# A vision tower on one NeuronCore: first attention with the query projections of two chunks in one set of matmuls

## The chip, the core and the metric

One core of a Trainium2 chip runs the whole program. The time is device microseconds of one execution; the median of several runs counts. The engines work side by side, each down its own list of instructions: TensorE (PE, matmuls; PEld is its weight load), VectorE (DVE), ScalarE (ACT), GpSimd (POOL), and SyncE (SP), which starts DMAs. An instruction waits for results of other engines by semaphores.

## The reference

The network takes 128 images, cuts each into 64 tokens of 256 features by two convolutions, and sends them through two layers of attention and feed-forward blocks. Only the attention of the first layer is touched:

```python
Q, K, V = x @ Wq.T, x @ Wk.T, x @ Wv.T            # x: (128, 64, 256), normalized
Qg = Q.reshape(B, L, 1, G, Dg)                    # G = 8 groups of Dg = 32
Kg = K.reshape(B, 1, L, G, Dg)
attn = einsum('bqkgd,d->bqkg', relu(Qg - Kg), w_mlp) + b_mlp[0]
attn = softmax(relu(attn), axis=2)
out = einsum('bqkg,bkdg->bqdg', attn, V.reshape(B, L, Dg, G))
```

The costly part is relu(q - k): for each image, each pair of a query and a key, and each of 256 features there is one subtraction and one relu, and then a weighted sum over 32 features.

## The kernel before, in words

Images are taken in eight blocks of 16 (NB = 16). A block's 64 queries per image are taken 8 at a time, so a block has eight chunks, and there are 64 chunks in all. I call a chunk by its place in its block, c0 to c7, which is its number modulo 8. Features lie on the partitions: 256 of them make two halves (hf = 0 and 1).

For one chunk, each of 16 images and each half, a tile of 8 queries x 64 keys is made, and three engines share that work. For images 0 to 7 of both halves, and 12 and 13 of half 1, VectorE takes max(q, k) (`larger`, L532; the missing -k is put in once per block as a key sum, L439 to L452, and enters through `begin`, L525). It reads the queries straight from their PSUM tile. For images 8 to 15 of half 0 and 8 to 11 of half 1, GpSimd subtracts (`difference`, L540) and ScalarE does the relu (L541). For images 14 and 15 of half 1 ScalarE does all of it, a query at a time (`by_query`, L550). GpSimd and ScalarE read the queries from a copy in SBUF that ScalarE makes (`queried`, L472). TensorE sums over features: each tile of 512 columns goes through one matmul with 32 output rows (`summed`, L342), four of them side by side, into the scores `sc`.

The scores of a chunk are finished in the course of the next chunk: VectorE takes their maximum and subtracts it (`less_max`, L566 to L568), ScalarE takes the exponent (L573), VectorE sums (L576), GpSimd scales (L580), TensorE transposes (L589), ScalarE copies (L597).

The order of all engines is written out by hand in one loop over the chunks, L696 to L757. It has named places (`do(n, "X")`, "A", "Y", "B", "Z", "O", "C", "W", "V1", "V2") into which other work is put by chunk number: the projections of the next block, the output of the last one. What matters here, in the order of a chunk on TensorE:

- the last sums of the chunk before, then the first sums of this one: three sets of four matmuls
- place X
- two more sets, which need the relu of the second difference
- the queries of the next chunk (`queries`, L454): four matmuls of 128 columns into a tile `pc`
- place Y
- three more sets, `begin` for the next chunk, the transposition, place Z.

In X are key projections (`keys`, L403, at c4 and c5) and value projections (`values`, L421, at c6 and c7), their copies on ScalarE at place A; a second set of values is in Y with copies at B, and key projections for the other eight images in Z.

Query tiles `pc` are in a pool of two PSUM buffers. A tile holds 2 x 16 x 8 queries, and 8 columns more into which `less_max` puts its maximum (L565). Parts from VectorE have a pool of three buffers of four images (`mvp`), differences one of five (`mgp`); projections and transposed tiles share four PSUM buffers (`sh.ps`).

Of the kernel before, what the change touches and what calls it, by code (L numbers as in the profile page):

```python
# [12 lines left out]
F32 = mybir.dt.float32  # L13
# [7 lines left out]
P = 128  # L21
B = 128
# [37 lines left out]
def bcast(ap, axis, n):  # L60

    v = ap.unsqueeze(axis)
    shape = list(v.shape)
    shape[axis] = n
    return v.to_broadcast(shape)
# [243 lines left out]
def relu_attention(c, sh, wqkv, wmlp, bmlp, beside):  # L309
# [6 lines left out]
    tc, nc, h2 = c.tc, c.nc, c.h2  # L316
    NB = 16
    NP = NB // 2
    np_, bp, atp, ep = sh.np_, sh.bp, sh.atp, sh.ep
    with (  # L320
# [29 lines left out]
        class Block:  # L350


            def __init__(self, b0):
                self.b0, self.p0 = b0, b0 // 2
                self.pc, self.q, self.ps = {}, {}, {}
# [97 lines left out]

            def queries(self, q0):  # L454

                self.pc[q0] = pc = psc.tile([P, 2 * NB * 8 + 8], F32, tag="pc", name="pc")
                pq = pc[:, : 2 * NB * 8].rearrange("p (c i t) -> p c i t", c=2, i=NB)
                xi = self.xT.rearrange("p c n (b t) -> p c (n b) t", b=2)
                for fo in range(2):
                    for fi in range(2):  # L460
                        nc.tensor.matmul(
                            pq[:, fo],
                            w[:, fi, fo * P : (fo + 1) * P],
                            xi[:, fi, :, q0 : q0 + 8],
                            start=(fi == 0),
                            stop=(fi == 1),
                        )

            def queried(self, q0):
                self.q[q0] = q = ep.tile([P, 2, NB // 2, 8], F32, tag="q", name="q")  # L470
                pq = self.pc[q0][:, : 2 * NB * 8].rearrange("p (c i t) -> p c i t", c=2, i=NB)
                nc.scalar.copy(q, pq[:, :, NB // 2 :])  # L472


            def outcome(self, hf):
# [36 lines left out]
        class Chunk:  # L512


            def __init__(self, blk, q0):
                self.blk, self.q0, self.parts, self.m = blk, q0, {}, {}
                self.pc = blk.pc.pop(q0)
                self.pq = self.pc[:, : 2 * NB * 8].rearrange("p (c i t) -> p c i t", c=2, i=NB)
                self.q = blk.q.pop(q0)

            def begin(self):
# [40 lines left out]
            def less_max(self):  # L562
                self.e = e = ep.tile([P, 8, T], F32, tag="e", name="e")
                self.mx = mx = ep.tile([P, 8], F32, tag="mx", name="mx")
                pm = self.pc[:, 2 * NB * 8 :]  # L565
                nc.vector.tensor_reduce(pm, self.sc, AX.X, ALU.max)  # L566
                nc.vector.tensor_scalar_max(mx, pm, 0.0)
                nc.vector.scalar_tensor_tensor(  # L568
                    e, self.sc, 0.0, bcast(mx, 2, T), ALU.max, ALU.subtract
                )  # L570
# [32 lines left out]
        def at(n, place, *steps):  # L603
            work.setdefault((n, place), []).extend(steps)

        def of(f, *a):
            return lambda: f(*a)
# [26 lines left out]
        for b, x in enumerate(blocks):  # L634
            n = 8 * b

            if b + 1 < len(blocks):
                at(n + 9, "X", of(x.outcome, 0))
                at(n + 9, "A", of(x.outcome_copied, 0, 0))
                at(n + 9, "B", of(x.outcome_copied, 0, 1))  # L640
                at(n + 9, "Y", of(x.outcome, 1))
                at(n + 9, "C", of(x.outcome_copied, 1, 0))
                at(n + 10, "O", of(x.outcome_copied, 1, 1))
                for i in range(4):
                    at(n + 10 + i // 2, "XY"[i % 2], of(x.back, i))
                    at(n + 10 + i // 2, ("V1", "V2")[i % 2], of(x.added, i))
            if b == 0:
                for i in range(4):
                    at(i // 2 * 2, "XY"[i % 2], of(x.values, i))
                    at(i // 2 * 2, "AB"[i % 2], of(x.valued, i))  # L650
                continue

            if b == 1:
                at(0, "V1", *(of(x.statistics, i) for i in range(NP)))
                at(0, "W", x.factors)
                at(0, "C", of(x.normal, 0), of(x.normal, 1))
                at(1, "X", of(x.transpose, 0))
                at(1, "A", of(x.normal, 2), of(x.transposed, 0))
                at(1, "B", of(x.normal, 3))
                at(1, "Z", of(x.transpose, 1))  # L660
                at(2, "O", of(x.transposed, 1))
            else:
                for i in range(NP):
                    at(n - 21 + i if b > 2 else 1 + i // 4, "V2", of(x.statistics, i))
                at(n - 15 if b > 2 else 2, "W", of(x.factors, 0, 4))
                at(n - 10, "W", of(x.factors, 4, 8))
                for i in range(4):
                    at(n - 12 + i, "C", of(x.normal, i))
                at(n - 8, "X", of(x.transpose, 0))
                at(n - 8, "A", of(x.transposed, 0))  # L670
                at(n - 8, "Z", of(x.transpose, 1))
                at(n - 7, "O", of(x.transposed, 1))
            for i in range(2):
                at(n - 6 + i, "A", of(x.normal, 4 + 2 * i))
                at(n - 6 + i, "B", of(x.normal, 5 + 2 * i))
                at(n - 6 + i, "Z", of(x.transpose, 2 + i))
                at(n - 5 + i, "O", of(x.transposed, 2 + i))
            for fo in range(2):
                at(n - 4 + fo, "X", of(x.keys, 0, fo))
                at(n - 4 + fo, "A", of(x.keyed, 0, fo))  # L680
                at(n - 4 + fo, "Z", of(x.keys, 1, fo))
                at(n - 3 + fo, "O", of(x.keyed, 1, fo))
            at(n - 2, "Y", x.key_sums)
            at(n - 1, "V1", x.correction)
            for i, (k, place) in enumerate(((6 - (b == 1), "Y"), (4, "Y"), (2, "X"), (1, "X"))):
                at(n - k, place, of(x.values, i))
                at(n - k, "BA"[place == "X"], of(x.valued, i))

        for (n, place), steps in beside.items():
            at(n, place, *steps)  # L690
# [5 lines left out]
        with tc.manual_schedule():  # L696
            seq = [(x, q0) for x in blocks for q0 in range(0, T, 8)]
            first(blocks[0])
            ch, old = Chunk(*seq[0]), None
            for n in range(len(seq)):  # L700
                new = None
                ch.difference(8, 0)
                ch.larger(mvp, 0, 4, 0)
                do(n, "O")
                if n == 0:
                    first_rest(blocks[0])
                    ch.begin()
                ch.by_query(14, 1, 0)
                ch.add(0, 0)
                do(n, "X")  # L710
                ch.difference(10, 0)
                ch.add(8, 0)
                ch.larger(mvp, 4, 4, 0)
                ch.add(4, 0)
                if old:
                    old.less_max()
                    old.exponents()
                ch.by_query(14, 1, 1)
                if n + 1 < len(seq):
                    seq[n + 1][0].queries(seq[n + 1][1])  # L720
                ch.difference(8, 1)
                do(n, "A")
                do(n, "V1")
                do(n, "Y")
                ch.difference(10, 1)
                if n + 1 < len(seq):
                    seq[n + 1][0].queried(seq[n + 1][1])
                    new = Chunk(*seq[n + 1])
                do(n, "B")
                ch.by_query(15, 1, 0)  # L730
                ch.add(8, 1)
                ch.larger(mvp, 0, 4, 1)
                ch.add(0, 1)
                if old:
                    old.sums()
                ch.difference(12, 0)
                if old:
                    old.weights()
                do(n, "W")
                ch.by_query(15, 1, 1)  # L740
                ch.larger(mvp, 4, 4, 1)
                ch.add(4, 1)
                if new:
                    new.begin()
                if old:
                    old.transpose()
                do(n, "Z")
                ch.larger(mgp, 12, 2, 1)
                do(n, "V2")
                ch.difference(14, 0)  # L750
                if old:
                    old.transposed()
                do(n, "C")
                ch.add(12, 0)
                ch.add(12, 1, True)
                old, ch = ch, new
            old.less_max()  # L757
# [1569 lines left out]
```

## Time and profile before

| | us |
|---|---|
| median of 3 runs | 2665.02 |
| the runs | 2665.02, 2655.38, 2665.51 |
| the profiled execution | 2654.66 |
| its span, first to last instruction | 2652.9 |
| first attention, about 195 to 1083 | 888 |

In the first attention a block of eight chunks takes about 110.3 us. These are its costliest groups there (line, engine, operation, what it writes and reads, count, busy time and mean ns of one, then idle time of the engine just before and who ended it):

```profile
L540 POOL TENSOR_TENSOR m<-q,k 128x1024 f32<-128x1024 f32 x384 | 719.6, 1907 | 55.9 <-PE sc L342 46.8 <-ACT q L472 8.9
L532 DVE TENSOR_TENSOR m<-pc,k 128x2048 f32<-128x2048 f32 x256 | 574.8, 2266 | 0.5 <-ACT q L472 0.5
L342 PE MATMUL sc<-m,wide 128*32 128x512 f32 x4096 | 520.0, 597 | 8.9 <-ACT m L541 6.6 <-DVE m L532 2.2
L541 ACT ACTIVATE m<-m 128x1024 f32<-128x1024 f32 x384 | 402.5, 1049 | 20.4 <-POOL m L540 20.4
L461 PE MATMUL pc<-xT,w 128*128 128x128 f32 x504 | 73.0, 288 | 0.0
```

A float32 matmul shows as two records, so a set of four matmuls is "x8" in a timeline, and four of 512 columns side by side take 0.86 us together, though each record is 597 ns long. In the timeline, the first number is the start in us and the second the time that the merged instructions cover; what stands in brackets is how long the engine idled before and which instruction of which engine ended that. The ends of matmuls are modelled, so PE's busy time is best read from one start to the next.

### The profile page before, as it was taken

To read this page: it belongs to the slowest core of one execution; us is meant where nothing else is said; L and a number is where in the kernel's file an instruction comes from. 1 tells how busy PE (TensorE), PEld (TensorE's weight loads), DVE (VectorE), ACT (ScalarE), POOL (GpSimd) and SP (SyncE) were. 2 spreads that over 40 slices of the span, in tenths; PEclk is the share of its full clock that TensorE was granted. 3 is DMA by queue.
4 is the path that set the end of the run, shared out by engine and by line. 5 is a ranking of instruction groups with operands and counts; after the bars stand their busy time and mean duration, and the time that the engine had idled before them with its cause. 6 is when DMAs were issued, how large, how long until landed. Compare 5 with 4: busy or idle time off the path is not lost. (4 is left out here: it accounts for less than half of the span.)

```text
span 2652.9 us, 81755 instructions
## 1 busy us (share of the span) xinstructions
PE 2526.2 (95%) x35633; PEld 1730.8 (65%) x35633; DVE 2012.2 (76%) x3000; ACT 1623.1 (61%) x3421; POOL 1625.8 (61%) x1428
## 2 busy tenths in 40 slices
PE   8989999999999999899999999999999877999997
PEld 4554444444444444688888888888566556888886
DVE  5759999999999999887878777878467786444443
ACT  2218889899898888666666666666344533233232
POOL 3319989899899999566565666653233313544544
PEclk9999999999999999999999999999999998999998
DMA  3100000000000000000000000000334444555554
GB/s 112 33 13 1 2 2 2 1 2 2 2 2 1 2 13 2 3 28 23 14 23 14 13 24 13 14 23 23 75 73 111 96 128 152 191 185 202 188 189 134
DMA packets 138046, 141.19 MB, mean 53 GB/s; under 512 B 108001, under 2 KB 121859, under 8 KB 129870
## 3 DMA queue, kind: packets, MB, share of 16 engines
q1 hardware_dynamic: 128684, 119.48, 15.3%
q0 software_dynamic: 7648, 14.77, 1.8%
q8 instruction: 281, 4.60, 0.7%
q10 hardware_dynamic: 1344, 1.61, 0.2%
q14 instruction: 89, 0.73, 0.1%
HBM read 104.00 MB, written 32.54 MB: 51 GB/s over the span
## 5 line engine op out<-in xcount | busy, mean ns | idle before, releaser
L540 POOL TENSOR_TENSOR m<-q,k 128x1024 f32<-128x1024 f32 x384 | 719.6, 1907 | 55.9 <-PE sc L342 46.8
L532 DVE TENSOR_TENSOR m<-pc,k 128x2048 f32<-128x2048 f32 (+1 forms) x320 | 646.3, 2055 | 0.5 <-ACT q L472 0.5
L342 PE MATMUL sc<-m,wide 128*32 128x512 f32 x4096 | 520.0, 597 | 8.9 <-ACT m L541 6.6
L541 ACT ACTIVATE m<-m 128x1024 f32<-128x1024 f32 x384 | 402.5, 1049 | 20.4 <-POOL m L540 20.4
L342 PEld LDWEIGHTS sc<-m,wide 128*32 128x32 f32 x4096 | 134.7, 109 | 269.2 <-issue 157.4
L550 ACT ACTIVATE m<-k,q 128x64 f32<-128x64 f32 x1024 | 270.8, 339 | 0.9 <-DVE k L419 0.9
L1070 DVE TENSOR_REDUCE mx<-sc 128x16 f32<-128x1024 f32 x128 | 156.0, 1219 | 133.6 <-PE sc L1058 133.6
L1085 POOL TENSOR_TENSOR e<-e,mx 128x1024 f32<-128x1024 f32 x127 | 241.6, 1903 | 9.9
L1017 ACT COPY kr<-pqk 128x512 f32<-128x512 f32 x254 | 137.9, 604 | 139.3 <-PE pqk L1011 139.3
L2153 PE MATMUL ph<-xt,w1s 128*128 128x256 f32 x896 | 200.5, 382 | 2.2 <-DVE xt L2144 1.5
L2169 PE MATMUL po<-w2s,hT 128*128 128x256 f32 x896 | 198.0, 379 | 0.0
L1084 POOL TENSOR_TENSOR mx<-mx,gate 128x16 f32<-128x16 f32 x127 | 27.4, 216 | 278.3 <-ACT z L1115 162.7
L2153 PEld LDWEIGHTS ph<-xt,w1s 128*128 128x128 f32 x896 | 171.0, 191 | 27.3 <-DVE xt L2144 2.1
L2169 PEld LDWEIGHTS po<-w2s,hT 128*128 128x128 f32 x896 | 168.1, 190 | 21.7
L1097 ACT COPY pT<-pt 128x512 f32<-128x512 f32 x256 | 138.8, 600 | 51.0 <-PE pt L1094 50.8
L1071 DVE TENSOR_TENSOR e<-sc,mx 128x1024 f32<-128x1024 f32 x128 | 156.7, 1224 | 4.4
L2187 POOL DMA_INDIRECT out<-y,rout x56 | 56.6, 1011 | 168.2 <-ACT hT L2157 129.2
L1077 DVE TENSOR_REDUCE mx<-e 128x16 f32<-128x1024 f32 x128 | 152.5, 1191 | 4.0 <-ACT e L1074 3.6
L2157 ACT ACTIVATE hT<-ph,w1s 128x256 f32<-128x256 f32 x224 | 93.0, 470 | 98.6 <-PE ph L2153 95.1
L1094 PE MATMUL pt<-ident,e 128*128 128x128 f32 x1024 | 141.3, 280 | 11.2 <-DVE vr L1047 7.0
L2174 ACT ACTIVATE y<-y,gf 128x256 f32<-128x256 f32 x56 | 28.0, 507 | 195.0 <-issue 110.3
L1074 ACT ACTIVATE e<-e 128x1024 f32<-128x1024 f32 x128 | 139.6, 1091 | 1.2 <-DVE e L1071 1.2
(337 smaller groups left out, 5009.4 us busy)
## 6 DMA issues: line engine op xcount, KB each, us to landing
w1s<-in_we SPq DMA_DIRECT2D x30, 1028.0 KB
w2s<-in_we SPq DMA_DIRECT2D x30, 1024.0 KB
h<-hd SPq DMA_DIRECT2D x4, 2048.0 KB
hx<-h SPq DMA_DIRECT2D x4, 2048.0 KB
out<-h SPq DMA_DIRECT2D x4, 2048.0 KB
xt<-in_x SPq DMA_DIRECT2D x15, 512.0 KB
hd<-h SPq DMA_DIRECT2D x15, 512.0 KB
x<-hd SPq DMA_DIRECT2D x12, 512.0 KB
```

The source lines that it names most:

```text
L342: nc.tensor.matmul(dst[j : j + 32], wide[:, hf, s : s + 32], part, start=start, stop=stop)
L532: nc.vector.tensor_tensor(m, bcast(self.pq[:, hf, i : i + n], 3, T), k, ALU.max)
L540: nc.gpsimd.tensor_tensor(m, bcast(self.q[:, hf, s : s + 2], 3, T), k, ALU.subtract)
L541: nc.scalar.activation(m, m, AF.Relu)
L550: nc.scalar.activation(self.parts[i, hf][:, q], self.blk.k[:, hf, i], AF.Relu, bias=self.q[:, hf, i - NB // 2, q : q + 1], scale=-1.0,)
L1070: nc.vector.tensor_reduce(mx, sc, AX.X, ALU.max)
L1071: nc.vector.tensor_sub(e, sc, bcast(mx, 2, T))
L1077: nc.vector.tensor_reduce(self.sm[x], self.e[x], AX.X, ALU.add)
L1085: eng.tensor_mul(e, e, bcast(sm, 2, T))
L1094: nc.tensor.transpose(pt[:, cq, :], e[:, i : i + 2, :].rearrange("p e s -> p (e s)"), c.ident)
L2153: nc.tensor.matmul(ph[:, j], self.w1[:, w0 : w0 + P], self.xt[:, fc], start=(fc == 0), stop=(fc == 1))
L2169: nc.tensor.matmul(po, self.hT[:, f, r * P : r * P + P], self.w2[:, f, :], start=(f == 0), stop=(f == 7))
```

## The change

- `queries` projects two chunks at once: still four matmuls per call, but of 2 x 128 columns, into one tile of 2 x 2 x 16 x 8 floats[...]. It runs at c0 (for c2 and c3), c3 (for c4 and c5), c5 (for c6 and c7) and c7 (for c0 and c1 of the next block) instead of in each chunk.
- `less_max` has no columns of its own any more. It puts its maximum on the first eight queries of its chunk, which VectorE has used by then.
- The copy `queried` of an odd chunk is issued in the even chunk before it, ahead of `less_max` and `exponents`. The copy of an even chunk stays where it was.
- `keys` of the first eight images move from X to Y and their copies from A to B, values of c6 and c7 likewise.

```diff
             def queries(self, q0):
-                self.pc[q0] = pc = psc.tile([P, 2 * NB * 8 + 8], F32, tag="pc", name="pc")
-                pq = pc[:, : 2 * NB * 8].rearrange("p (c i t) -> p c i t", c=2, i=NB)
-                xi = self.xT.rearrange("p c n (b t) -> p c (n b) t", b=2)
+                pc = psc.tile([P, 2, 2, NB, 8], F32, tag="pc", name="pc")
+                for k in range(2):
+                    self.pc[q0 + 8 * k] = pc[:, k]
+                xi = self.xT.rearrange("p c n (b s k t) -> p c s k (n b) t", b=2, k=2, t=8)
                 for fo in range(2):
                     for fi in range(2):
                         nc.tensor.matmul(
-                            pq[:, fo],
+                            pc[:, :, fo],
                             w[:, fi, fo * P : (fo + 1) * P],
-                            xi[:, fi, :, q0 : q0 + 8],
+                            xi[:, fi, q0 // 16],
...
             def less_max(self):
...
-                pm = self.pc[:, 2 * NB * 8 :]
+                pm = self.pq[:, 0, 0]
...
             for fo in range(2):
-                at(n - 4 + fo, "X", of(x.keys, 0, fo))
-                at(n - 4 + fo, "A", of(x.keyed, 0, fo))
+                at(n - 4 + fo, "Y", of(x.keys, 0, fo))
+                at(n - 4 + fo, "B", of(x.keyed, 0, fo))
...
-            for i, (k, place) in enumerate(((6 - (b == 1), "Y"), (4, "Y"), (2, "X"), (1, "X"))):
-                at(n - k, place, of(x.values, i))
-                at(n - k, "BA"[place == "X"], of(x.valued, i))
+            for i, k in enumerate((6 - (b == 1), 4, 2, 1)):
+                at(n - k, "Y", of(x.values, i))
+                at(n - k, "B", of(x.valued, i))
...
                 ch.larger(mvp, 4, 4, 0)
                 ch.add(4, 0)
+                if n % 2 == 0:
+                    seq[n + 1][0].queried(seq[n + 1][1])
                 if old:
                     old.less_max()
                     old.exponents()
                 ch.by_query(14, 1, 1)
-                if n + 1 < len(seq):
-                    seq[n + 1][0].queries(seq[n + 1][1])
+                two = {0: 2, 3: 1, 5: 1, 7: 1}.get(n % 8)
+                if two and n + two < len(seq):
+                    x, q0 = seq[n + two]
+                    x.queries(q0)
...
                 if n + 1 < len(seq):
-                    seq[n + 1][0].queried(seq[n + 1][1])
+                    if n % 2:
+                        seq[n + 1][0].queried(seq[n + 1][1])
                     new = Chunk(*seq[n + 1])
```

More of the change, by code (lines that the diff above doesn't have):

```diff
@@ L470, in queried @@
                 self.q[q0] = q = ep.tile([P, 2, NB // 2, 8], F32, tag="q", name="q")
-                pq = self.pc[q0][:, : 2 * NB * 8].rearrange("p (c i t) -> p c i t", c=2, i=NB)
-                nc.scalar.copy(q, pq[:, :, NB // 2 :])
+                nc.scalar.copy(q, self.pc[q0][:, :, NB // 2 :])
             def outcome(self, hf):
@@ L516, in __init__ @@
                 self.blk, self.q0, self.parts, self.m = blk, q0, {}, {}
-                self.pc = blk.pc.pop(q0)
-                self.pq = self.pc[:, : 2 * NB * 8].rearrange("p (c i t) -> p c i t", c=2, i=NB)
+                self.pq = blk.pc.pop(q0)
                 self.q = blk.q.pop(q0)
```

## The prediction, made before the changed kernel ran

> **What bounds the kernel now.** I read the busy shares first, then the first attention's own stretch by windows, then the timeline of each engine over one block of eight chunks (527 to 638 us), then the list of waits. "c0" to "c7" are the chunk numbers modulo 8.
>
> ```profile
> PE 2526.2 (95%) x35633; PEld 1730.8 (65%) x35633; DVE 2012.2 (76%) x3000; ACT 1623.1 (61%) x3421; POOL 1625.8 (61%) x1428
> ...
> 527.00:638.00 111.00, 110.49 (x1276) 50.69 (x1279) 104.92 (x102) 99.97 (x228) 101.97 (x66) 1.00 0.01 2
> ```
>
> The change lives in the first attention alone, 195 to 1083 us. There PE shows 99% (second column of the window's row; then weight loads, DVE, ACT, POOL), but DVE has 95%, POOL 92% and ACT 90% as well: four engines are nearly full, and a chunk is as long as the slowest of them in that chunk. So I looked at where DVE, which carries the chunk's rhythm through the maximum over the scores (L566), waits:
>
> ```profile
> 604.53 0.70 DVE L566 TENSOR_REDUCE pc<-sc 128x8 f32<-128x512 f32 x1 [1.97 <-PE sc L342]
> 618.84 0.70 DVE L566 TENSOR_REDUCE pc<-sc 128x8 f32<-128x512 f32 x1 [1.38 <-PE sc L342]
> 631.79 0.70 DVE L566 TENSOR_REDUCE pc<-sc 128x8 f32<-128x512 f32 x1
> ...
> DVE pc L566 <- PE sc L342: 27.2, 25, 3.0
> ```
>
> In each block DVE waits for the scores 1.97 us after c4 and 1.38 after c5 (the chunks with key projections), 0.78 after c2, 0.20 after c1 (timeline at 575.59 and 560.68), and nothing after c0, c3, c6, c7: 4.33 of about 110.3 us. The last line is the list of waits for 300 to 960 us; over the whole stage the instructions on the query buffer waited 37.1 us for these matmuls (the view of that tile). That is the ceiling of what a faster PE can give: 1.4% of the kernel. In the four other chunks DVE runs without a gap, and ACT and POOL run close behind it.
>
> The second thing to see is that a busy PE isn't always working. This is c7, PE and then ACT:
>
> ```profile
> 629.60 3.00 PE L342 MATMUL sc<-m,wide 128*32 128x512 f32 x24
> 632.53 1.99 PE L426 MATMUL pv<-w,xT 128*128 128x256 f32 x8
> 634.46 1.92 PE L342 MATMUL sc<-m,wide 128*32 128x512 f32 x16
> 636.31 1.16 PE L461 MATMUL pc<-xT,w 128*128 128x128 f32 x8
> 637.40 2.92 PE L342 MATMUL sc<-m,wide 128*32 128x512 f32 x24
> ...
> 628.72 1.06 ACT L541 ACTIVATE m<-m 128x1024 f32<-128x1024 f32 x1 [1.08 <-POOL m L540]
> 632.60 1.05 ACT L541 ACTIVATE m<-m 128x1024 f32<-128x1024 f32 x1
> ```
>
> The second group of scores needs the relu that ACT ends at 633.65. PE gets there at 634.46 only because a values projection (pv, 1.93 us from start to start) stands in between: it fills time in which PE would wait anyway. Where that place ("X") holds only a short transposition, the wait shows: in c0 the same group takes 2.64 us (535.23 to 537.87) instead of 1.85 (634.46 to 636.31).
>
> [...] Today the next chunk's queries lie in another buffer than those DVE reads, and the trace agrees: DVE waited for a query copy once, 0.5 us, at the start. [...]
>
> **The change part by part.**
>
> *Queries for two.* A chunk's queries are 4 matmuls, 1.09 us from start to start alone (636.31 to 637.40) and 0.99 with another projection behind (593.13 to 594.12). For two chunks they stream 256 columns each; the values projection is such a set and takes 1.93. Per block: 8 x 1.09 go, 4 x 1.93 come: -1.0 us of PE. But c1, c2, c4, c6 lose 1.0 to 1.1 each and c0, c3, c5, c7 gain 0.84.
>
> *Keys and values from X to Y*, behind the queries: [...] about 0.1 us of fill goes per joint (1.93 against 1.82, 594.12 to 595.94), and the two runs of scores become one, another 0.13 (five groups of 0.86). The copies to SBUF move behind the second difference on ACT; nobody needs them before the next block.
>
> *Where PE then waits.* In place of X nothing covers the relu.
> - c4: PE 15.87 us now (586.64 to 602.51). Queries -1.0, joints -0.23: 14.65. But the relu ends at 590.09 and the scores get there at 589.23: +0.86. 15.5, so 0.35 is won.
> - c5: 14.32 now; queries +0.84, joints -0.23: 14.9. Its relu is in time. 0.6 is lost, and c5 isn't hidden, since DVE waits there. c4 and c5 together: +0.2.
> - c6: -1.1 queries, but its end is set by POOL (628.72, the 1.08 above): 0.
> - c7: the first run ends at about 632.3, the relu at 633.65: 1.3 us idle; then 1.75 scores, 1.93 queries, 1.82 values, 2.6 + 1.1 + 1.1: c0 starts at 643.9 instead of 642.19, +1.7. DVE's maximum follows PE's start of a chunk by 2.02 us where PE is late (602.51 and 604.53), so 642.19 could have served it at 644.21, and it came at 644.83: 0.62 of slack. DVE waits 1.1 new.
> - c0: queries +0.84 lie under the wait for relu (today 650.56, c0 of the next block). But ACT's transposed copy waits for PE, so ACT is 1.7 late, DVE 1.1.
> - c1, c2: -1.0 each. c1's end hangs on POOL's last difference, so only 0.2 comes; in c2 the 0.78 goes wholly, DVE's own 14.13 us is late next. About -0.9.
> - c3: +0.84, under 1.0 us that PE waits for DVE (sc from 580.44 takes 3.56 to the next start, not 2.6): 0.
>
> *Two chunks in one bank.* The built program shows two waits that the diff doesn't: in even chunks the early copy waits for DVE's second maximum, and DVE's third (L532, "larger") waits for the copy; in odd chunks the maximum over scores waits for DVE's own last read of that bank. The latter ends an overlap: L532's pairs start 0.08 us before the one ahead ends, while a dependent step (604.53+0.70 to 605.33) starts 0.10 behind: 0.18 in odd chunks, in c7, c1, c3 on the path where DVE doesn't wait otherwise. For the former the copy (0.25 us) stands behind the relu: in c4 and c6 it ends 0.9 us before DVE needs it; in c0 at 536.15 where DVE starts at 536.17, no slack; in c2 about 0.3 late against its DVE time. With ACT 1.7 and DVE 1.1 late in c0 by the step above, DVE waits 0.65 there, with the 2.28 maximum, and the sums and POOL's weights behind it. That wait makes c2's vanish, since DVE comes later there.
>
> *The copy's move itself* frees 0.15 of ACT in odd places and falls into ACT's waits for DVE (25.6 us at L573, 300 to 960): 0. *Start:* the first queries take 0.86 more, before DVE's and POOL's first work (POOL waited 8.89 for that copy): +0.85 once.
>
> *Sum per block:* c7 and c0 to c1's maximum +1.95 (1.1 PE, 0.65 copy, 0.18 odd), c1 and c2 -0.8 with c3's 0.18 in it, c4 and c5 +0.2: about +1.3. Seven block ends: +9; start +0.85; odd chunks of the first block +0.3; the last block has no keys, gains about 0.6. **+9.5 us.** The profiled execution is 2654.66 (span 2652.9): 2664. The three runs shown are 2655.38, 2665.02 and 2665.51, so it stands at their lower end, 10.4 below the median. I put the change on the middle, 2660: **2669**.
>
> Unknown costs: the matmul over two runs of 128 columns isn't in the trace; at 1.7 (columns alone) it saves 0.25 a time, at 2.2 (twice the old) it costs as much: -4 to +4 us over 16 uncovered ones. The copy's wait: 0 if ACT keeps up, up to one relu (1.05) in each of 16 even chunks c0 and c2: 0 to 17, I take 0.65 in c0.
>
> **The rivals.**
> - *PE is the bound throughout.* Then every saved PE time counts: -1.0 queries and four joints of 0.23 a block, 8 blocks: -15 us, 2640 on the profile, 2645 on the middle. For it: PE's 99%, and both waits after c4 and c5. Against: DVE gapless in half the chunks, and the relu times above. 0.17.
> - *DVE pays for the bank.* One mechanism: the early copy sits behind a relu that waits for POOL, and DVE's third maximum behind the copy. It decides as soon as ACT ends the copy later than 1.6 us after L566's start; c0 has no slack and c2 is past it. At one relu in two of four even chunks, 16 x 1.05 = 17 us on the 9.5 less the 4.5 already in it: +22, 2682. For it: c0's margin of 0.02. Against: c4, c6. 0.28.
> - *Cancelled*: the bank's waits cost nothing and c7's hole is refilled by PE's lead from c6: -0.9 and +0.2 a block, -4: 2656 (within 0.5%, with the forecast). 0.12.
>
> **How the numbers follow.** 0.5% is 13 us, about what a measurement of this kernel can tell. Forecast 0.43, of which 0.09 runs past +13; cancelled 0.12. Faster 0.17; slower 0.28 + 0.09 = 0.37; same 0.46. The range takes in the second rival and the joint costs, and most of the first: 2646 to 2688.
>
> **What would show it.** Right: in c7 the two score runs around the missing values take over a microsecond longer than 4.4; L566 in c0 waits about 1.1 for the scores, where it waited for nothing; L532 has ACT q as a releaser, around 0.6 in c0; the 0.78 after c2 gone; after c4 about 1.6 and after c5 about 2.0. Queries at 1.93. Wrong: if the idle before L566 falls below 25 us with no new waits at L532, PE was the bound and the kernel is faster; if L532 waits for ACT in c2, c4 or c6 too, the second rival holds.

## The result and the profile after

Over 14 runs each, the changed kernel took 2671.14 us in the median (2668.57 to 2678.02) and the kernel before 2660.94 us (2655.18 to 2665.86; the three runs of the table above are among these, and their median of 2665.02 was high). The ratio is 1.0037, with a 95% interval from 1.0028 to 1.0046: 10 us slower. The profiled execution of the changed kernel took 2672.7 us with a span of 2670.7.

That span is 17.8 us longer than the one before, more than the runs differ. Between the first and the last maximum over scores, which frame the first attention, 866.51 us became 877.29, so 10.8 of the 17.8 lie there and 1.7 ahead of it. The remaining 5.3 are in code behind it that the change doesn't touch. From the last of these maxima to the end the profile before took 1570.4 us, this one 1575.7, and those of the experiments below between 1573.1 and 1586.3, so this part varies from profile to profile by more than 5.3. So I read single profiles by the attention's own length, and whole kernels by the ratio of runs.

The busy shares hardly move. In the same window of 111 us (the row's second number is PE, the fourth DVE) PE is busy half a microsecond less than before (109.98 against 110.49) and DVE 1.1 less (103.81 against 104.92):

```profile
PE 2533.4 (95%) x35377; PEld 1721.5 (64%) x35377; DVE 2014.4 (75%) x3000; ACT 1622.2 (61%) x3421; POOL 1626.0 (61%) x1428
...
527.00:638.00 111.00, 109.98 (x1234) 49.05 (x1233) 103.81 (x101) 98.22 (x222) 100.49 (x64) 1.00 0.01 2
```

To see where the time went, I took the starts of the maximum over the scores (L566 before, L567 after) and subtracted each from the next. Column c0 runs from the maximum issued in c0 to the next one, which is over c0's own scores and issued in c1. In brackets stands how long DVE waited for those scores. All are us, in one steady block, which begins at 424.31 before and at 428.88 after:

| | c0 | c1 | c2 | c3 | c4 | c5 | c6 | c7 | sum |
|---|---|---|---|---|---|---|---|---|---|
| before | 12.97 | 13.14 (0.20) | 14.91 (0.78) | 14.05 | 14.89 (1.97) | 14.32 (1.38) | 12.94 | 13.04 | 110.26 |
| after | 13.65 | 12.95 | 14.50 | 14.04 | 14.59 (1.66) | 14.71 (1.79) | 13.03 | 13.94 (0.81) | 111.41 |
| difference | +0.68 | -0.19 | -0.41 | -0.01 | -0.30 | +0.39 | +0.09 | +0.90 | +1.15 |

The loss is in two neighbouring chunks, c7 and c0. This is the timeline of DVE in the next block (its intervals agree within 0.02 with those of the table, but for c0), with the maxima over the scores of c4 to c7, and a line of the c0 that follows:

```profile
610.38 0.70 DVE L567 TENSOR_REDUCE pc<-sc 128x8 f32<-128x512 f32 x1 [1.65 <-PE sc L342]
625.09 0.70 DVE L567 TENSOR_REDUCE pc<-sc 128x8 f32<-128x512 f32 x1 [1.78 <-PE sc L342]
638.13 0.70 DVE L567 TENSOR_REDUCE pc<-sc 128x8 f32<-128x512 f32 x1
652.06 0.70 DVE L567 TENSOR_REDUCE pc<-sc 128x8 f32<-128x512 f32 x1 [0.81 <-PE sc L342]
654.27 2.29 DVE L532 TENSOR_TENSOR m<-pc,k 128x2048 f32<-128x2048 f32 x1 [0.52 <-ACT q L473]
```

The fourth line is a wait where there was none, at the end of c7; the fifth is the new wait for the early copy. Where the former comes from is in c7's timeline on PE, then on ACT:

```profile
634.99 4.06 PE L342 MATMUL sc<-m,wide 128*32 128x512 f32 x28
639.90 1.91 PE L342 MATMUL sc<-m,wide 128*32 128x512 f32 x12 [0.84 <-ACT m L541]
641.74 1.99 PE L463 MATMUL pc<-xT,w 128*128 128x256 f32 x8
643.57 1.89 PE L426 MATMUL pv<-w,xT 128*128 128x256 f32 x8
645.39 2.78 PE L342 MATMUL sc<-m,wide 128*32 128x512 f32 x24
...
650.04 2.78 PE L342 MATMUL sc<-m,wide 128*32 128x512 f32 x24
```

```profile
634.97 1.06 ACT L541 ACTIVATE m<-m 128x1024 f32<-128x1024 f32 x1 [1.33 <-POOL m L540]
...
638.80 1.04 ACT L541 ACTIVATE m<-m 128x1024 f32<-128x1024 f32 x1
```

From 634.99 to 641.74 five groups of scores take 6.75 us. In c5 of the same block, where nothing stands between them either and the relu is in time, they take 4.51 (608.36 to 612.87), so 2.24 are waits. The rows above show only 0.84 of that as idle, since a merged row covers short waits inside it as if they were work. The rows of the weight loads, one for each matmul record, show the waits better (the same stretch):

```profile
636.07 0.16 PEld L342 LDWEIGHTS sc<-m,wide 128*32 128x32 f32 x8 [0.94 <-ACT m L541]
...
639.89 0.16 PEld L342 LDWEIGHTS sc<-m,wide 128*32 128x32 f32 x8 [1.75 <-ACT m L541]
```

There are two holes. The first ends at 636.07, when the relu of c6's last difference is there (634.97 + 1.06 = 636.03). PE is there early, 3.14 us ahead of the maximum in c7 (638.13) where it was 2.19 (629.60 and 631.79), now that c6 has no queries. The second ends at 639.89, with the relu of c7's second difference, which ends at 638.80 + 1.04 = 639.84: this is where the values stood. Then the doubled queries (1.83 from start to start) and the values follow, with nothing in their way. PE starts on the sums of c0 11.91 us after the maximum issued in c7 (650.04 and 638.13), where before it was 10.40 (the row below and 631.79):

```profile
642.19 2.78 PE L342 MATMUL sc<-m,wide 128*32 128x512 f32 x24
```

The same is seen in the costliest groups (DVE's third maximum, then the score matmuls; behind the last bar the engine's idle time before them). ScalarE now holds up DVE for 6.1 us in the whole kernel where it was 0.5, and PE's rows show 12.9 us of waits for relus where it was 6.6 (the numbers of before are in the list of costliest groups in "Time and profile before"):

```profile
L532 DVE TENSOR_TENSOR m<-pc,k 128x2048 f32<-128x2048 f32 (+1 forms) x320 | 646.6, 2056 | 6.1 <-ACT q L473 6.1
L342 PE MATMUL sc<-m,wide 128*32 128x512 f32 x4096 | 530.9, 599 | 15.4 <-ACT m L541 12.9
```

### The profile page after: what moved, and what is told of

The parts are those of the page before. It is cut to its first block, busy times and chain, and to the rows that moved or that the text cites. A ratio compares the mean times of both kernels' runs of the same rounds, so it can differ in the third digit from the quotient of the medians.

```text
span 2670.7 us, 81337 instructions
## 1 busy us (share of the span) xinstructions
PE 2533.4 (95%) x35377; PEld 1721.5 (64%) x35377; DVE 2014.4 (75%) x3000; ACT 1622.2 (61%) x3421; POOL 1626.0 (61%) x1428
## 3 DMA queue, kind: packets, MB, share of 16 engines
q0 software_dynamic: 7648, 14.77, 1.7%
## 5 line engine op out<-in xcount | busy, mean ns | idle before, releaser
L342 PE MATMUL sc<-m,wide 128*32 128x512 f32 x4096 | 530.9, 599 | 15.4 <-ACT m L541 12.9
L1102 PE MATMUL pt<-ident,e 128*128 128x128 f32 x1024 | 141.2, 280 | 10.6 <-DVE vr L1055 6.1
```

The source lines that it names most:

```text
L342: nc.tensor.matmul(dst[j : j + 32], wide[:, hf, s : s + 32], part, start=start, stop=stop)
L1102: nc.tensor.transpose(pt[:, cq, :], e[:, i : i + 2, :].rearrange("p e s -> p (e s)"), c.ident)
```

## The experiments

My theory is that of the prediction: c7 loses its filler and c0 is late behind it, with a small price for the shared bank (the PSUM tile `pc` with the queries of two chunks). The rivals are PE's total (fewer query matmuls, less time), the doubled queries by themselves, and the bank's price as the main cost. Each ratio is to runs of the kernel before beside it. "Block" is the sum of the eight intervals as in the table, "stage" is first to last maximum.

### The moves alone

The kernel before, with its queries chunk by chunk, but keys and values in Y:

```diff
-                at(n - 4 + fo, "X", of(x.keys, 0, fo))
-                at(n - 4 + fo, "A", of(x.keyed, 0, fo))
+                at(n - 4 + fo, "Y", of(x.keys, 0, fo))
+                at(n - 4 + fo, "B", of(x.keyed, 0, fo))
...
-                at(n - k, place, of(x.values, i))
-                at(n - k, "BA"[place == "X"], of(x.valued, i))
+                at(n - k, "Y", of(x.values, i))
+                at(n - k, "B", of(x.valued, i))
```

> Before, with only the keys and values moved from X to Y and their copies from A to B; queries stay one chunk at a time. Measured by the time between the maxima over scores of one block of eight chunks (before 110.26 us, after 111.39). My theory (X covered PE's wait for a relu): the wait for scores after c4 grows from 1.97 to about 2.6, after c5 falls from 1.38 to about 1.1, c7 grows by 0.2 and c0 by 0.3 to 0.5: block 111.0 to 111.3, whole stage +6 us. Rival (PE is the bound throughout): joints saved, block about 109.8, -4 us.

Measured: 2666.37 us, ratio 1.0026 (1.0014 to 1.0038). Stage 870.65, block 110.89 (+0.63), a little below the range expected. The maxima that end c4 and c5 on DVE's timeline:

```profile
607.87 0.70 DVE L566 TENSOR_REDUCE pc<-sc 128x8 f32<-128x512 f32 x1 [2.55 <-PE sc L342]
621.75 0.70 DVE L566 TENSOR_REDUCE pc<-sc 128x8 f32<-128x512 f32 x1 [0.95 <-PE sc L342]
```

c4's wait rose by 0.58 and c5's fell by 0.43, from the same move of the same matmuls. In c5 the relu is in time and the move only saves joints (in the profile before, a set of queries took 0.99 us from start to start with another projection behind it and 1.09 without; what makes the difference wasn't shown). In c4 it isn't, and the hole shows on PE's timeline, the row of c4 first and then that of c5, each with the queries behind it:

```profile
589.40 5.41 PE L342 MATMUL sc<-m,wide 128*32 128x512 f32 x40
594.75 1.16 PE L461 MATMUL pc<-xT,w 128*128 128x128 f32 x8
...
605.85 4.58 PE L342 MATMUL sc<-m,wide 128*32 128x512 f32 x40
610.36 0.82 PE L461 MATMUL pc<-xT,w 128*128 128x128 f32 x5
```

The same five groups take 5.35 us in c4 and 4.51 in c5, and PE's rows mark neither with an idle time. Again the weight loads of c4 show it:

```profile
592.90 0.16 PEld L342 LDWEIGHTS sc<-m,wide 128*32 128x32 f32 x8 [0.78 <-ACT m L541]
```

So "behind the queries" isn't better or worse in itself, it depends on whether PE reaches the relu early. That PE's total counts everywhere falls: this kernel has the same matmuls with fewer joints and is slower.

### The pairs alone

The changed kernel, with keys and values back in their old places:

```diff
-                at(n - 4 + fo, "Y", of(x.keys, 0, fo))
-                at(n - 4 + fo, "B", of(x.keyed, 0, fo))
+                at(n - 4 + fo, "X", of(x.keys, 0, fo))
+                at(n - 4 + fo, "A", of(x.keyed, 0, fo))
...
+            for i, (k, place) in enumerate(((6 - (b == 1), "Y"), (4, "Y"), (2, "X"), (1, "X"))):
+                at(n - k, place, of(x.values, i))
+                at(n - k, "BA"[place == "X"], of(x.valued, i))
```

> After, with keys and values back in X and A; pairs of queries and the early copy stay. My theory: after c4 the wait for scores falls to about 1.0, after c5 it grows to about 2.2, c1 and c2 gain 0.6 together, c7 loses 0.2, the third maximum of VectorE waits for the copy about 0.5 in c0: block 110.0 to 110.5, no change against before within 0.2%. Rival (the shared bank is what costs): the block stays at 111.4. Rival (PE the bound): block 109.3.

Measured: 2665.50 us, ratio 1.0012 (1.0003 to 1.0022). Stage 870.22, block 110.56 (+0.30). DVE after c4, after c5, and in c0:

```profile
605.60 0.70 DVE L567 TENSOR_REDUCE pc<-sc 128x8 f32<-128x512 f32 x1 [1.38 <-PE sc L342]
620.57 0.70 DVE L567 TENSOR_REDUCE pc<-sc 128x8 f32<-128x512 f32 x1 [2.04 <-PE sc L342]
...
648.85 2.29 DVE L532 TENSOR_TENSOR m<-pc,k 128x2048 f32<-128x2048 f32 x1 [0.52 <-ACT q L473]
```

c4 wins 0.59 and c5 loses 0.65, c1 and c2 win 0.54 and c0 loses 0.68. c7 stays at 13.04. The block is 0.85 shorter than in the changed kernel, with all of the shared bank left in, so the bank isn't the main cost.

The wait of 0.52 in c0 is here too, though DVE isn't held up in c7. So it doesn't hang on c7's hole. The timelines point to the doubled queries: with 0.84 more of them in c7, PE starts c0's sums 2.03 us ahead of the maximum in c0 (644.62 and 646.65), where before it was 2.64 (642.19 and 644.83). ScalarE's copy of the transposed weights waits for PE (0.58 us there, 0.36 before), and the relu of the second difference, behind which the early copy stands, ends later against that maximum. These are the maximum in c0 and that relu, before, with the pairs alone, and, for the relu, in the changed kernel (its maximum is the one at 652.06 above):

```profile
644.83 0.69 DVE L566 TENSOR_REDUCE pc<-sc 128x8 f32<-128x512 f32 x1
645.20 1.04 ACT L541 ACTIVATE m<-m 128x1024 f32<-128x1024 f32 x1
...
646.65 0.69 DVE L567 TENSOR_REDUCE pc<-sc 128x8 f32<-128x512 f32 x1
647.63 1.04 ACT L541 ACTIVATE m<-m 128x1024 f32<-128x1024 f32 x1
...
653.04 1.05 ACT L541 ACTIVATE m<-m 128x1024 f32<-128x1024 f32 x1
```

The relu ends 1.41 us behind the maximum before, 2.02 with the pairs alone and 2.03 in the changed kernel. No run isolates this step.

### Values of c7 back in X

The changed kernel, with one set of values per block in its old place:

```diff
-            for i, k in enumerate((6 - (b == 1), 4, 2, 1)):
-                at(n - k, "Y", of(x.values, i))
-                at(n - k, "B", of(x.valued, i))
+            for i, (k, place) in enumerate(((6 - (b == 1), "Y"), (4, "Y"), (2, "Y"), (1, "X"))):
+                at(n - k, place, of(x.values, i))
+                at(n - k, "BA"[place == "X"], of(x.valued, i))
```

> After, with only c7's values back in X (their copy in A). My theory: the hole before c7's relu is filled again, c7 falls from 13.93 to about 13.05 with no wait for scores, everything else stays as in after: block 110.5 to 110.8 against 111.5, stage -6 us. Rival (c7 is longer because of the 0.84 us of a second chunk's queries): c7 stays at 13.8 or above.

Measured: 2665.63 us, ratio 1.0015 (1.0006 to 1.0024). Stage 870.15, 7.1 less than in the changed kernel; c7 is 13.04 again with no wait, the block 110.52. PE in c7:

```profile
629.74 3.87 PE L342 MATMUL sc<-m,wide 128*32 128x512 f32 x24
633.53 1.99 PE L426 MATMUL pv<-w,xT 128*128 128x256 f32 x8
635.46 1.92 PE L342 MATMUL sc<-m,wide 128*32 128x512 f32 x16
637.31 1.99 PE L463 MATMUL pc<-xT,w 128*128 128x256 f32 x8
```

The values fill the time up to the second relu, and the second run of scores takes 1.85 us. The first hole is still there (3.79 us from the first row to the second, for three groups that take 2.71 in the c0 behind it) and so are the doubled queries, 1.93 from start to start; neither costs DVE anything in c7. The copy of the values has moved along with them, but that isn't what helps: the second relu starts 0.68 us behind the maximum in c7 (633.55 and 632.87), in the changed kernel 0.67 (638.80 and 638.13). The rival that blames the queries by themselves for c7 falls, as do the moves by themselves, which cost 0.27 in c7: it takes both for 0.90. Of the 7.1 in the stage, I take 1.47 for a one-off of the changed kernel's profile (last section); then 5.7 of the remaining 9.3 us that the change costs in the attention hang on where this one projection stands. The ratios of runs agree: 1.0037 and 1.0015 are 5.9 us apart.

### The maximum in SBUF

Meant to price the wait of DVE for its own last read of the query bank, by taking the maximum out of that bank:

```diff
-                pm = self.pq[:, 0, 0]
+                pm = ep.tile([P, 8], F32, tag="pm", name="pm")
```

> After, with the maximum over scores written to a small SBUF tile instead of onto used queries in the shared bank. My theory: in odd chunks the reduction no longer waits for VectorE's own last read of the bank; 0.18 us less in c2 to c3's maximum and in c7's, block 111.0 against 111.39. Rival (such a wait costs nothing): 111.4.

Measured: 2699.83 us, ratio 1.0147 (1.0130 to 1.0164), stage 905.46. A gain was expected; this is 29 us slower than the changed kernel. The line behind the maximum, which clips 128 x 8 numbers at zero, has become slow (its own view, shortest/median/longest in ns):

```profile
L568 DVE TENSOR_SCALAR mx<-pm x64: 171/654/1752, 218.4 to 1123.9; 128x8 f32<-128x8 f32 x64
```

In the changed kernel the same line reads from PSUM:

```profile
L568 DVE TENSOR_SCALAR mx<-pc x64: 165/166/168, 218.4 to 1095.8; 128x8 f32<-128x8 f32 x64
```

And in the timeline of the SBUF kernel it stands beside GpSimd's subtractions:

```profile
574.17 9.36 POOL L540 TENSOR_TENSOR m<-q,k 128x1024 f32<-128x1024 f32 x5
...
579.98 1.71 DVE L568 TENSOR_SCALAR mx<-pm 128x8 f32<-128x8 f32 x1
```

The operation went from 0.166 us to as long as 1.752, about one GpSimd subtraction (1.91), while the tensor_reduce ahead of it, now also writing to SBUF, took 0.69 as before (0.70). In all the line took 57.6 us in the attention where it took 10.6, more than the 29 us that the kernel lost. What made it slow was not shown by any run. The bank's price couldn't be read from this run.

### The early copy ahead of the relu

In even chunks, the copy issued before the relu of the second difference instead of behind it (`difference` gets a third argument, False, that leaves its relu out):

```diff
...
-                ch.difference(10, 0)
-                ch.add(8, 0)
+                m = ch.difference(10, 0, False)
                 ch.larger(mvp, 4, 4, 0)
-                ch.add(4, 0)
                 if n % 2 == 0:
                     seq[n + 1][0].queried(seq[n + 1][1])
+                nc.scalar.activation(m, m, AF.Relu)
+                ch.add(8, 0)
+                ch.add(4, 0)
```

> After, with the early copy put ahead of the relu of the second difference on ScalarE instead of behind it. My theory: the waits of L532 for the copy (0.52 in c0, 0.18 in c2 of each block) vanish; the scores that need the relu come 0.15 later; c0 falls from 13.64 to about 13.3 since PE is late next, c2 by 0.18: block about 110.9. Rival (the copy's wait is not on the path): 111.4 with the waits moved to the scores.

Measured: 2674.20 us, ratio 1.0057 (1.0040 to 1.0074), stage 877.70, block 112.05, where 110.9 was expected. c0 went from 13.65 to 13.34 and c2 from 14.50 to 14.23, and DVE waits for the copy in neither. But c4 went from 14.59 to 15.51. ACT there:

```profile
595.86 0.27 ACT L473 COPY q<-pc 128x128 f32<-128x128 f32 x1 [0.66 <-DVE m L532]
596.02 1.06 ACT L718 ACTIVATE m<-m 128x1024 f32<-128x1024 f32 x1
```

The copy waits 0.66 us for DVE's second read of the bank, and now the relu stands behind it (line 718 is that relu in this kernel). PE gets its scores late, and DVE waits 2.59 us after c4 instead of 1.65. So which of the two goes first has a different right answer in different chunks: in c0 and c2 DVE comes first and waits for the copy, in c4 ACT comes first and waits for DVE.

### The early copy left in its old place

One look at the price of the bank when nothing hides it: the pairs, but with all copies at the end of a chunk.

```diff
-                if n % 2 == 0:
-                    seq[n + 1][0].queried(seq[n + 1][1])
...
                 if n + 1 < len(seq):
-                    if n % 2:
-                        seq[n + 1][0].queried(seq[n + 1][1])
+                    seq[n + 1][0].queried(seq[n + 1][1])
```

> After, with the odd chunk's query copy at its old place behind the fourth difference. If the shared bank orders VectorE behind that copy as the program's waits say, VectorE's third maximum in every even chunk waits some 4 us for ACT q, and the kernel is 80 to 130 us slower. If reads of a bank by two engines are not ordered, nothing changes against after.

Measured: 2809.48 us in the one profiled run, 147 above the median of the kernel before beside it (2662.00). In the view of the copy's line, DVE's maxima waited 123.7 us for it, 32 times:

```profile
who waited for it (us, times):
  DVE m L532: 123.7, 32
```

That is 3.9 us in each even chunk, as expected: with two chunks in one bank, DVE's third maximum in this program stands still until ACT has copied the other chunk. The kernel lost more than the 80 to 130 us expected. Besides the waits, PE's granted clock was lower, in the mean 0.969 against 0.989 in the profile before; how much of the 147 us that is was not isolated. This is what the early copy, which looks like a detail of the change, holds down to 0.52 and 0.18 us.

### A mix of both

The changed kernel with each piece where its own chunk wants it: keys of c4 in X and of c5 in Y, values of c7 in X and of c6 in Y, the copy ahead of the relu in c0 and c2, behind it in c4 and c6.

```diff
-                at(n - 4 + fo, "Y", of(x.keys, 0, fo))
-                at(n - 4 + fo, "B", of(x.keyed, 0, fo))
+                at(n - 4 + fo, "XY"[fo], of(x.keys, 0, fo))
+                at(n - 4 + fo, "AB"[fo], of(x.keyed, 0, fo))
...
+            for i, (k, place) in enumerate(((6 - (b == 1), "Y"), (4, "Y"), (2, "Y"), (1, "X"))):
+                at(n - k, place, of(x.values, i))
+                at(n - k, "BA"[place == "X"], of(x.valued, i))
...
+                if n % 8 in (0, 2):
+                    seq[n + 1][0].queried(seq[n + 1][1])
+                nc.scalar.activation(m, m, AF.Relu)
+                if n % 8 in (4, 6):
+                    seq[n + 1][0].queried(seq[n + 1][1])
```

> After, with c4's keys and c7's values back in X, and the early copy ahead of the relu in c0 and c2 alone (behind it in c4 and c6). My theory: c0 13.3, c1 13.0, c2 14.2, c3 14.05, c4 14.3, c5 14.7, c6 and c7 13.05: block 109.7, which is 0.6 below before; stage about 863 against 866.5. Rival (any kernel with two chunks in a bank loses): block above 110.3.

Measured: 2659.37 us, ratio 0.9988 (0.9977 to 0.9999). Stage 864.14, 13.2 below the changed kernel (11.7 without the one-off) and 2.4 below the kernel before; block 109.66. All that the pairs win in c1, c2 and c4 is kept (12.95, 14.23, 14.31), and c7 is 13.04. Its median is the lowest of all kernels here, but only 0.12% below the kernel before, with an interval that nearly touches 1.

### Keys a chunk sooner

What is left is c4 and c5, where DVE waits 1.38 and 1.78. The mix once more, with the key projections at c3 and c4 instead of c4 and c5:

```diff
-                at(n - 4 + fo, "XY"[fo], of(x.keys, 0, fo))
-                at(n - 4 + fo, "AB"[fo], of(x.keyed, 0, fo))
+                at(n - 5 + fo, "YX"[fo], of(x.keys, 0, fo))
+                at(n - 5 + fo, "BA"[fo], of(x.keyed, 0, fo))
```

> The mix, with the keys of the first eight images a chunk sooner: one set in Y of c3, the other in X of c4, none of them in c5. My theory: c3 14.05 (PE has about 1 us of slack there), c4 about 15.1, c5 about 13.2: block 108.8, stage about 857, which is 0.35% faster than before. Rival (PE's total is what counts, not its place): no change against the mix.

Measured: 2661.82 us, ratio 0.9991 (0.9979 to 1.0003), block 109.81, no gain. DVE after c3, c4 and c5:

```profile
591.14 0.70 DVE L569 TENSOR_REDUCE pc<-sc 128x8 f32<-128x512 f32 x1 [0.22 <-PE sc L342]
606.11 0.70 DVE L569 TENSOR_REDUCE pc<-sc 128x8 f32<-128x512 f32 x1 [2.02 <-PE sc L342]
619.94 0.70 DVE L569 TENSOR_REDUCE pc<-sc 128x8 f32<-128x512 f32 x1 [0.90 <-PE sc L342]
```

The three intervals are 14.40, 14.97 and 13.84, in sum 43.21, against 14.05, 14.31 and 14.71 or 43.07 in the mix. The wait only moved, and the gain of 0.35% that I expected didn't come. That fits the rival: with no hole left in these three chunks, it seems to be the sum of PE's work over them that counts.

## Why the prediction was right

It said 2669, 9 above a middle of 2660, and 2671.14 was measured, 10.2 above 2660.94. The main step was right as a mechanism. The closeness of the sum is in part luck. By its own steps:

*c7's missing filler*: right, and shown by putting the values back (c7 -0.90). Predicted was that PE comes 1.7 late to c0 and DVE waits 1.1; PE came 1.51 late (11.91 against 10.40) and DVE waited 0.81. That PE, without queries in c6, would also stand in c7 for the relu of c6's last difference wasn't foreseen; by the run with the values back it costs nothing in c7.

*c4 and c5*: waits of 1.6 and 2.0 predicted, 1.65 and 1.78 measured; together +0.09 against +0.2. The opposite signs of the moves in the two chunks (+0.59 and -0.44) and of the pairs (-0.59 and +0.65) were each seen alone. For the pairs alone I had expected a wait of 1.0 after c4; it was 1.38.

*The bank's waits*: the copy in c0 0.52 against 0.65, right in size, but the prediction tied it to the missing filler (ScalarE 1.7 late, DVE 1.1). It came without a wait of DVE in c7 (pairs alone), where PE and ScalarE already were 0.6 later against DVE, and it went when the copy stood ahead of the relu. That c2's wait would vanish was wrong: 0.18 stayed. The overlap lost in odd chunks shows as predicted where no wait for scores covers it, in the maximum at 638.13 (shown above; the one before is at 644.83). These are the instructions of DVE ahead of the two, before first:

```profile
640.46 4.45 DVE L532 TENSOR_TENSOR m<-pc,k 128x2048 f32<-128x2048 f32 x2
...
633.57 4.46 DVE L532 TENSOR_TENSOR m<-pc,k 128x2048 f32<-128x2048 f32 x2
```

Before, the maximum starts 0.08 ahead of the end of its predecessor (640.46 + 4.45 = 644.91), now 0.10 behind it (638.03): the step of 0.18 that was taken. But there was less to lose: in c7 the maximum before already started 0.02 behind (631.79 against 627.32 + 4.45), and c6, the interval that it ends, grew by 0.09. In c2, by the run with the copy ahead of the relu, it is 0.10 (14.23 against 14.91 - 0.78, which has no overlap in it). The price wasn't isolated by a run of its own.

*c1 and c2*: -0.60 measured against -0.8. *c3*: nothing, as said. *c6*: +0.09 against nothing.

*Queries for two*: 1.93 us alone and 1.83 with values behind, as the values' row had suggested. The 1.7 for the columns alone is an estimate that follows from the scores: four matmuls of 512 columns side by side take 0.86 us there, so four of 256 one behind another would take 1.72. At the start they take 0.84 more (1.73 against 0.89 from start to start), as said; the other 0.9 of the 1.7 us ahead of the first maximum lie elsewhere.

*The sum*: +1.15 in the block shown against about +1.3. Six inner blocks came to +6.5 in all, the first to +1.44. (In one of the six, c0 is 14.02, with an idle time of 0.47 of DVE that stays unexplained; the runs with the pairs alone and with the values back have it in the same block.) The last block was put at -0.6 and measured +2.84, so that term was wrong even without the 1.46 of the one-off: c5 was 0.85 longer there and c2 0.35, and both come with the pairs (14.14 and 14.77 with the pairs alone, 13.27 and 14.41 with the moves alone). So too small a loss in the last block made up for too large a one in the others.

*Rivals*: PE as the bound throughout falls for the change as a whole (the moves alone and the changed kernel both give PE less to do and take longer), but fits c3 to c5 once no hole is left there. The prediction's sign for it was less than 25 us of waits for scores between 300 and 960 us with no new waits for the copy. The waits did fall, from 27.2 to 23.6, but new ones for the copy came:

```profile
DVE pc L567 <- PE sc L342: 23.6, 20, 3.1
```

DVE paying for the bank was real at a small size in c0 and c2. By the letter of the prediction a wait in c2 was to speak for that rival; but at 0.18, and 6.1 us for all such waits in the kernel, it is far from one relu in two of four even chunks. Its large form needs the copy late (147 us).

## What to carry to other kernels

Work that an engine has to do anyway can cost nothing right ahead of an instruction that waits for another engine, as the values did in c7 (13.04 us with them in X, 13.94 without). Taking it from there to a place where it costs less by itself can lose more than it saves: the moves alone made the block 0.63 us longer. The waits to look at are also those inside merged rows that look busy (1.75 us by the weight loads where the row showed 0.84). The answer belongs to each chunk, not to the loop body: the same move was right in c5 (0.44 shorter) and wrong in c4 and c7 (0.59 and 0.27 longer). Whoever puts the data of two chunks into one PSUM tile should find the copy that opens it for the next engine and see how much slack it has in each chunk: here DVE waited 0.52 us in c0 and 0.18 in c2 with the copy early, 3.9 in each even chunk with it late.

## What the hardware showed unexpectedly

A VectorE operation on 128 x 8 numbers went from 0.166 us with its input in PSUM to a median of 0.654 and up to 1.752 us with its input in SBUF, beside GpSimd's subtractions, and the kernel with 64 of them was 1.1% slower than with PSUM (2699.83 against 2671.14). The size of this operation said little of what it cost there.

In the last block of the changed kernel's profile the granted PE clock (third from the end in a row of windows) fell to 0.61 and 0.54 for some 4 us, the only time in that stage:

```profile
1045.00:1047.00 2.00, 1.53 (x10) 0.43 (x12) 2.00 (x2) 2.00 (x6) 2.00 (x2) 0.61 0.00 0
1047.00:1049.00 2.00, 2.00 (x12) 0.48 (x10) 2.00 (x2) 2.00 (x6) 2.00 (x2) 0.54 0.00 0
```

c4 of that block took 14.53 us, against 13.07 in the profile before. It took 13.06 or 13.07 in the profiles of the moves, the pairs, the values in X, the copy ahead of the relu, the mix and the keys a chunk sooner. PE stands idle for 1.83 us ahead of the dip, but for as long at the same place of the run with the values in X, where 18 score records then take 2.34 us that take 3.81 in the dip. So I put 1.46 of the stage's 10.8 us down to a chance of this profile. No second profile of the changed kernel tests that, and why the clock fell is open.
